# A hand-written order for three streams: six new lists, and a held period at the last image border

## The chip, the cores and the metric

The kernel runs on one core of one Trainium2 chip. The metric is the device time of one execution in microseconds; less is better. Engines are named as in the profile: PE (TensorE matmuls, with PEld for its weight loads), DVE (VectorE), ACT (ScalarE), POOL (GpSimd) and SP (SyncE, which here only issues DMAs).

## The reference

The input x is 4 images of 256 x 256 positions with 64 channels, float32. Layer 0 mixes in the frequency domain and then convolves; layer 1 works along the rows' axis (T = 256).

```python
h  = pw(ln(x, g1, b1), w_te, b_te)                      # 64 -> 128
F  = fft2(h, axes=(1, 2))
fc = gelu(pw(concat([real(F), imag(F)]), w_fc, b_fc))   # 256 -> 256
sp = real(ifft2(fc[..., :128] + 1j * fc[..., 128:], axes=(1, 2)))
x1 = x + pw(sp, w_tp, b_tp)                             # 128 -> 64
h2 = pw(ln(x1, g2, b2), w_fe, b_fe)                     # 64 -> 128
d  = gelu(depthwise3x3(h2, w_dw) + b_dw)
x2 = x1 + pw(d, w_fp, b_fp)                             # 128 -> 64
trend = moving_average(x2, 25)
xf = rfft(x2 - trend, axis=1)[:, :128]
ys = einsum('bmnc,cmk->bknc', xf, w_real + 1j * w_imag)
out = trend + irfft(pad(ys), n=256, axis=1)
```

## The kernel before

Layer 0 runs as three streams that overlap, each a few steps behind the one before it; what one image's stream leaves goes through DRAM to the next.

- The forward stream takes 32 column groups of each image: layer norm and the Fourier transform along the rows. Its operations are `fl` (load), `fq fr fR fm fM fA fB fC fp fx` (statistics, the root, scaling), `fa fb fh0 fh1` (sums and differences on DVE and POOL; `fh` is L609), `y0 y1` (transform on PE, L615), `yt0 yt1` (evictions on ACT and the store `y_d`).
- The spectral stream takes 65 row pairs of each image, two per period: `x xs` (second transform, L725 and L740), `m` (mixing matmuls with `wp`, L750), `gc b g` (copy on ACT L764, sums on DVE L770, activation on ACT L775), `p` (sums on POOL, L781), `z zs w zt` (product with `w_tp` and inverse transform, L805 to L833), `u us uc uf` (the inverse along the other axis, L856 to L920, and the store `u_d`, L896).
- The convolution stream takes 32 column chunks of each image: `ul UL xl XL cl` (loads), `c0 cc` (column sums on DVE; c0 is L990), `s` (inverse along the rows, L1041), `r0 r1` (residual, L1054 and L1062), `cq cr cR cm cM cA cB cC cp cx` (second layer norm; cx is L410), `t tt T Ta` (transpose and row sums; tt is L1098 to L1100 on ACT, T is L1124 to L1132 on POOL), the convolution's products, its combination, `a` (activation on ACT, L1276), `o fs ft st` (last product L1283, its eviction, the turn back L1308, residual and store).

The 3 x 3 convolution is done as six products over row and column combinations. `gm` issues the first of them (L1166): eight matmuls into two single PSUM banks `ps_h_c`, and then eight into a tile of two banks, `ps_hh_c`, of which there is one. `em` issues the rest: eight matmuls into two more single banks. `gh` and `eh` add the half-height products (L1180). The results are taken out by `gc_0 gc_1` (ACT, L1209 and L1212) and `cf0 cf1` (DVE, L1233 to L1245) for gm, and by `ec0 ec1` (ACT copies, L1200) with `sp0 sp1` (POOL sums, L1218 and L1223) for em. The last op of `cf1`, L1245, frees the two-bank tile. A chunk that comes late (`is_late`, from the period LATE_CHUNKS on) takes another path for em: `ce0 ce1`, DVE sums straight from PSUM (L1258, L1260). There are eight PSUM banks: six single ones, which are handed round between all operations in the order of issue, and the two-bank tile.

The order of work is written by hand and not left to a scheduler: PE, DVE, ACT and POOL run their instructions in exactly the order in which the program issues them, and SP issues the DMAs in that order. Before period S0 = 35, 17 turns of the list FIRST run the forward stream beside layer 1's matrix preparation (`v vc mm mt`, per-channel matrices that join moving average, transform and mixing). Then `period(n)` walks one list for n = 35 to 207: SPECTRUM to n = 71, FULL while all three streams run (72 to 131), MIXED when the forward stream has ended (132 to 170), and CONV when only the convolution remains (171 to 207). At the end `layer1` applies the matrices m_d to x2.

An entry `em:-4` means: issue `em` for chunk n - 4 in this period. `do(op, index)` first issues what the operation follows (FOLLOWS, EARLY) and what frees a bank for it, so an entry can pull others ahead of it, and one whose work was pulled before issues nothing. A chunk of the convolution has as its index the period in which it starts, given by `chunk_at`: 72 to 103 for the first image, 105 to 136, 137 to 168 and 170 to 201 for the others. At 104 and 169 there is no chunk, since an image's convolution needs the spectral stream's last rows; the empty index runs through the stages of the pipeline from period to period.

```python
    for b in range(B):
        at = max(at, S0 + opened(b) + 2 + LATE)
        for q in range(COLS):
            chunk_at[at] = (b, q)
            at += 1
    END = at + 6
```

Of the kernel before, what the change touches and what calls it, by code (L numbers as in the profile page):

```python
# [136 lines left out]
def conv_seq_kernel(ctx: ExitStack, tc: tile.TileContext, a: dict, tables: bass.AP, out: bass.AP):  # L137
    nc = tc.nc
    x = a["x"]
    B = x.shape[0]  # L140
# [27 lines left out]
    def make_room(op):  # L168

        for other in list(taken):  # L170
            if len(free_banks) >= NEEDS.get(op, 1):
                break
            if other in taken:
                holder, k = taken[other][1]
                late = holder == "em" and k >= LATE_CHUNKS
                releaser = "ce1" if late else RELEASES[holder]
                if (releaser, k) not in pulling:
                    pulling.append((releaser, k))
                    do(releaser, k)
                    pulling.pop()  # L180
# [1352 lines left out]
    S0 = FWD + 3  # L1533
    LATE = 1

    def opened(b):

        return (KH * (b + 1) + 2) // 2 + 1

    chunk_at, at = {}, 0  # L1540
    for b in range(B):
        at = max(at, S0 + opened(b) + 2 + LATE)
        for q in range(COLS):
            chunk_at[at] = (b, q)
            at += 1
    END = at + 6
    place = {chunk: at for at, chunk in chunk_at.items()}
    CONV_FROM = S0 + LATE + opened(B - 1) + 3

    def is_late(j):  # L1550
        return place[j] >= LATE_CHUNKS

# [42 lines left out]
    MIXED = numbered("""
        xl:-1 XL:-1 ft0:-6 zs:-5 st0:-6 ft1:-6 st1:-6 em:-4 g0:-3 T1:-3 Ta:-3 eh:-4 zt:-6 ec0:-4
        ec1:-4 m1:-3 sp0:-5 sp1:-5 cx:-2 w:-5 cf1:-5 gc1:-3 g1:-4 b1:-3 cm:-1 cc:-2 UL t0:-2 a0:-5
        xs:-1 zt:-5 gm:-4 t1:-2 tt0:-2 a1:-5 p0:-4 p1:-4 z:-4 zs:-4 gh:-4 uf:-3 cM:-1 p0:-3 gc_0:-4
        cf0:-4 g1:-3 cp:-1 m1:-2 gc1:-2 b1:-2 s cl tt1:-2 r0 gc_1:-4 m0:-2 gc0:-2 m0:-1 p1:-3 z:-3
        gc0:-1 r1 x b0:-2 xs o1:-5 fs1:-5 u:-2 o0:-5 T0:-2 x:1 cq b0:-1 us:-2 fs0:-5 g0:-2 cr cR  # L1600
        uc:-2 w:-4 ul:1
    """)

    CONV = numbered("""
        ce0:-5 ul:-1 s:-1 cl:-1 xl:-1 XL:-1 r0:-1 ce1:-5 r1:-1 a0:-5 ft0:-6 st0:-6 cr:-1 gm:-4
        ft1:-6 a1:-5 cq:-1 Ta:-3 cR:-1 o1:-5 o0:-5 gh:-4 st1:-6 t0:-2 gc_0:-4 fs0:-5 gc_1:-4 t1:-2
        cm:-1 cc:-2 cM:-1 cp:-1 cf0:-4 tt1:-2 cf1:-4 tt0:-2 em:-4 eh:-4 T0:-2 T1:-2 cx:-1 fs1:-5 UL
    """)
# [14 lines left out]
    PAIRS = set("x xs m0 m1 gc0 gc1 b0 b1 g0 g1 p0 p1 z zs w zt".split())
    BACK = {"u", "us", "uc", "uf"}
# [11 lines left out]
    def do(op, index):  # L1636

        if op not in ops:
            return
        for k in range(done.get(op, -1) + 1, index + 1):  # L1640
            for other, at in EARLY.get(op, ()) if k < LATE_CHUNKS else ():
                do(other, k + at)
            for other, at in follows.get(op, ()):
                do(other, k + at)
            if op in ("u", "zt") and ring[0](op, k):
                do(*ring[0](op, k))
            if op in ("fq", "cq", "cc") and sq_user:
                user = sq_user[-1][0]
                do(user, done[user[0] + "q"])
            if op in RELEASES:  # L1650
                make_room(op)
            if done.get(op, -1) >= k:
                continue
            done[op] = k
            busy.append((op, k))
            if op in PAIRS:
                if op == "x" and k < B * KH - 2:
                    do("yt0", (k + 3) // KH * FWD + FWD - 1)
                    do("yt1", (k + 3) // KH * FWD + FWD - 1)
                if k < B * KH:  # L1660
                    ops[op](k)
            elif op in BACK:
                ops[op](k)
            elif op in MATRICES:
                if k < C:
                    ops[op](k)
            elif op in HALF_MATRICES:
                if k < 2 * BESIDE:
                    ops[op](k)
            elif op in forward:  # L1670
                if k < B * FWD:
# [30 lines left out]
    with in_order, ExitStack() as right:  # L1702
        with (
# [3 lines left out]
            forward = forward_h(fwd)  # L1707
# [92 lines left out]
```

## Time and profile before

| | |
|---|---|
| median of 3 runs | 4286.83 us (4285.57 to 4288.68) |
| profiled execution | 4282.18 us |
| its span, first to last instruction | 4280.0 us |
| PE / DVE / ACT / POOL busy | 4123.3 / 3453.5 / 2962.3 / 3174.2 us |
| mean granted clock of PE | 0.987 |
| HBM traffic | 364.81 MB read, 286.00 MB written |

By stage (us from the start of the span; the border stages are those where one image's convolution gives way to the next):

| stage | from - to | length | PE busy |
|---|---|---|---|
| FIRST and fill | 0 - 340 | 340 | 304.0 |
| SPECTRUM | 340 - 780 | 440 | 437.8 |
| convolution comes in | 780 - 963 | 183 | 160.5 |
| FULL | 963 - 1628 | 665 | 660.0 |
| border at n = 104 | 1628 - 1852 | 224 | 205.1 |
| FULL | 1852 - 2381 | 529 | 526.7 |
| end of the forward stream, border at n = 137 | 2381 - 2577 | 196 | 183.1 |
| MIXED | 2577 - 3194 | 617 | 613.9 |
| last border | 3194 - 3419 | 225 | 187.8 |
| CONV | 3419 - 3798 | 379 | 376.7 |
| layer 1 | 3798 - 4280 | 482 | 467.7 |

A steady period takes 26.5 us in FULL, 23.6 in MIXED and 13.8 in CONV. In a row of the profile "x8" is the number of instructions in the group, the time in brackets is the idle time of that engine just before it, and the name after the arrow is what it waited for.

### The profile page before, as it was taken

How to read it: one execution, taken by the hardware profiler on the slowest of the kernel's cores; microseconds unless marked ns; L12 is line 12 of the kernel's file. 1: busy time of each engine (PE TensorE's matmuls, PEld its weight loads, DVE VectorE, ACT ScalarE, POOL GpSimd, SP SyncE). 2: the span in 40 equal slices, each digit the busy share in tenths (PEclk: the TensorE clock that was granted, in tenths of full speed). 3: DMA queues.
4: the chain of work that ended last, by engine and by line, in shares of the span. 5: the costliest groups of instructions: out<-in, count | busy, mean ns of one | idle time of the engine just before them, and what ended most of it. 6: DMA issues, size and time to landing. Idle time of an engine off the chain costs nothing.

```text
span 4280.0 us, 67389 instructions
## 1 busy us (share of the span) xinstructions
PE 4123.3 (96%) x22443; PEld 2329.5 (54%) x22443; DVE 3453.5 (81%) x5234; ACT 2962.3 (69%) x5409; POOL 3174.2 (74%) x3156
## 2 busy tenths in 40 slices
PE   8999999889999999899999999999998899999999
PEld 4544444345555555455555556666665566654444
DVE  6968999889999999899999878888886799962222
ACT  3438988778888887788888777888885466641221
POOL 6869999789999988899988877888886688840000
PEclk9999999999999999999999999999999999999999
DMA  6664555535555545445554333444433544439895
GB/s 192 213 192 132 158 159 165 170 99 138 139 138 138 138 138 141 125 132 140 141 141 133 100 106 101 110 108 123 109 99 101 165 114 114 118 109 368 344 342 226
DMA packets 763904, 655.26 MB, mean 153 GB/s; under 512 B 46413, under 2 KB 657695, under 8 KB 755240
## 3 DMA queue, kind: packets, MB, share of 16 engines
q1 hardware_dynamic: 726696, 583.84, 47.0%
q10 hardware_dynamic: 36864, 67.13, 4.1%
q8 instruction: 180, 2.95, 0.3%
q14 instruction: 164, 1.34, 0.1%
HBM read 364.81 MB, written 286.00 MB: 152 GB/s over the span
## 4 chain that ended last, share of the span: by engine, by line
PE 47%; DVE 8%; DMA 2%; POOL 2%; ACT 1%; issue 1%; SPq 0%; DVEq 0%; POOLq 0%; ACTq 0%
PE ps_o L1504 9%; PE ps_h_c L1166 5%; PE ps_p L750 4%; PE ps_h_c L1180 4%; PE ps_f_c L1283 4%; PE ps_s_c L1041 3%; PE ps_hh_c L1166 3%; PE ps_z L805 3%; PE ps_u L856 2%; PE ps_x L725 2%; PE ps_t_c L1088 2%; PE ps_ft_c L1308 2%; PE ps_hh_c L1180 2%; PE ps_zt L823 1%; PE ps_y L615 1%
## 5 line engine op out<-in xcount | busy, mean ns | idle before, releaser
L770 DVE TENSOR_TENSOR g<-ps_p,g 128x512 f32<-128x512 f32 x1040 | 703.0, 683 | 127.7 <-ACT g L764 109.4
L781 POOL TENSOR_TENSOR g<-g 128x512 f32<-128x512 f32 (+1 forms) x520 | 674.1, 1312 | 92.8 <-ACT g L775 84.9
L775 ACT ACTIVATE g<-g,b_fc 128x1024 f32<-128x1024 f32 (+1 forms) x520 | 595.2, 1145 | 1.7 <-DVE g L770 1.6
L750 PE MATMUL ps_p<-xs,wp 64*128 64x512 f32 (+1 forms) x2080 | 562.2, 615 | 7.0 <-DVE g L770 3.8
L1166 PE MATMUL ps_h_c<-td,wc_main 128*128 128x256 f32 x2048 | 500.5, 387 | 3.7 <-DVE g L770 1.4
L1504 PE MATMUL ps_o<-xc,mt 128*128 128x512 f32 x1024 | 441.2, 594 | 2.6 <-DVE oc L1518 2.6
L1166 PEld LDWEIGHTS ps_h_c<-td,wc_main 128*128 128x128 f32 x2048 | 372.6, 192 | 99.3 <-issue 32.1
L764 ACT COPY g<-ps_p 128x512 f32<-128x512 f32 (+1 forms) x520 | 298.5, 589 | 163.3 <-PE ps_p L750 80.7
L1276 ACT ACTIVATE h_c<-h_c,b_conv 128x1024 f32<-128x1024 f32 x256 | 296.5, 1160 | 158.1 <-DVE h_c L1245 53.8
L1518 DVE TENSOR_SCALAR oc<-ps_o,b_fp 128x512 f32<-128x512 f32 x128 | 93.6, 749 | 348.0 <-DMA out_dram<-oc 177.4
L1516 ACT ACTIVATE oc<-ps_o,b_fp 128x512 f32<-128x512 f32 x128 | 86.4, 686 | 359.4 <-PE ps_o L1504 202.8
L1128 POOL TENSOR_TENSOR td<-tt 128x512 f32<-128x512 f32 x256 | 326.9, 1298 | 10.0
L1504 PEld LDWEIGHTS ps_o<-xc,mt 128*128 128x128 f32 x1024 | 194.9, 191 | 248.3 <-issue 236.2
L609 POOL TENSOR_TENSOR xb<-xt 128x512 f32<-128x512 f32 x224 | 284.9, 1279 | 54.9 <-DVE xt L602 36.6
L750 PEld LDWEIGHTS ps_p<-xs,wp 64*128 64x128 f32 x2080 | 191.7, 186 | 235.7 <-issue 84.2
L805 PE MATMUL ps_z<-g,w_tp 128*64 128x512 f32 x1024 | 284.7, 616 | 25.8 <-POOL g L781 13.9
L1322 DVE TENSOR_TENSOR st<-x_c,ps_ft_c 128x256 f32<-128x256 f32 x512 | 260.5, 599 | 36.9 <-PE ps_ft_c L1308 36.8
L725 PEld LDWEIGHTS ps_x<-tab,yb 128*64 128x64 f32 x4064 | 232.7, 137 | 95.7 <-issue 38.3
L1180 PE MATMUL ps_h_c<-td,wc_half 64*128 64x256 f32 (+1 forms) x2048 | 278.9, 396 | 2.3 <-POOL td L1132 1.0
L615 PE MATMUL ps_y<-xb,tab 128*64 128x512 f32 x1024 | 270.6, 614 | 10.8 <-POOL xb L609 9.2
L1283 PE MATMUL ps_f_c<-h_c,w_fp 128*64 128x512 f32 x1024 | 266.1, 614 | 15.2 <-ACT h_c L1276 15.2
L1041 PE MATMUL ps_s_c<-uc_c,tab 64*128 64x512 f32 x1024 | 260.4, 612 | 16.6 <-DVE uc_c L990 11.2
(201 smaller groups left out, 9588.2 us busy)
## 6 DMA issues: line engine op xcount, KB each, us to landing
y_d<-yt SPq DMA_DIRECT2D x256, 256.0 KB, 3.6
yb<-y_d SPq DMA_DIRECT2D x256, 256.0 KB, 4.2
u_d<-ut SPq DMA_DIRECT2D x256, 256.0 KB, 3.6
x_c<-in_x_dram SPq DMA_DIRECT2D x512, 128.0 KB, 3.6
x_d<-st SPq DMA_DIRECT2D x128, 512.0 KB, 5.1
xc<-x_d SPq DMA_DIRECT2D x64, 1024.0 KB, 8.3
out_dram<-oc ACTq DMA_DIRECT2D x256, 256.0 KB, 5.7
xt<-in_x_dram SPq DMA_DIRECT2D x504, 128.0 KB, 2.5
```

What stands on the lines that cost most here:

```text
L725: nc.tensor.matmul(ps[r * C : (r + 1) * C, j * N + t * P : j * N + (t + 1) * P], blk[:, t, k, r * C : (r + 1) * C], tb[:, t, :], start=Tru ...
L750: nc.tensor.matmul(ps[:, :nf], wp[rows, cols], rhs[rows], start=True, stop=r == 1 or not pr["special"],)
L770: nc.vector.tensor_tensor(gt[:, i], re, gt[:, 1], op)
L775: nc.scalar.activation(g, g, AF.Gelu, bias=b_fc[:, half : half + 1])
L781: nc.gpsimd.tensor_tensor(g[:, 0], g[:, 0], g[:, 1], op)
L805: nc.tensor.matmul(ps[r * C : (r + 1) * C, :nf], w_tp, d[:, :nf], start=True, stop=True)
L1041: nc.tensor.matmul(pss[i], tb[i * C : (i + 1) * C], uc[i * C : (i + 1) * C, ::-1, 1 - r, :] if down else uc[i * C : (i + 1) * C, :, r, :], ...
L1128: tt_(new[:, k : k + 3 : 2], a_c, nb_e, op)
L1166: nc.tensor.matmul(product(j, k, par), wc_main[:, par, k, :], td[:, k, slots(j)].rearrange("p j q -> p (j q)"), start=k in (0, 1, 3), stop ...
L1180: nc.tensor.matmul(product(j, k, par)[:, dst.start * Q : dst.stop * Q], wc_half[lo : lo + C, k, :], td[lo : lo + C, k, src].rearrange("p j ...
L1283: nc.tensor.matmul(ps[par * C : (par + 1) * C], w_fp, gs[j][:, :, par, i0 : i0 + 2, :].rearrange("p r j q -> p r (j q)"), start=True, stop ...
L1504: nc.tensor.matmul(ps[:, :nf], mts[i // CM][:, i % CM, t, to * P : (to + 1) * P], xc[:, t, :, :, i, :], start=t == 0, stop=t == 1,)
```

## The change

The six lists are given in another order; most entries that move are not neighbours of what they were. Two things beside that: at n = 168 (HOLDS) the convolution is held for a period, which closes the gap at index 169, so that the last image's chunks are 169 to 200 and every convolution operation from n = 168 on uses n - 1 as its base; and LATE_CHUNKS becomes 166 for 167. END stays 208. A period's list in n = 168 then issues only what is left of the spectral stream.

On PE the order of FULL's instructions differs in one place: `em` of a chunk is issued ahead of `gm` of the same chunk and not after it. In MIXED and CONV it is as before, in SPECTRUM y0 and y1 change places. On the other engines: in FULL `cA` moves behind `zt` on ACT, the first pair of `p` ahead of `fh1` and `fx` ahead of `sp1` on POOL, `XL` ahead of `cl` on SP; in MIXED `Ta` and `xs` move earlier and one `zt` later on ACT, `sp0` ahead of `T1` on POOL, `ul` from the end of the period to its start on SP; in CONV `ft0` and `cR` move by a few places; in FIRST `fq`, `fR` and the `yt` stand elsewhere among ACT's. At n = 104 `UL:1` and `y1:-3` stand later in FULL, and so do `u`, `uc` and `uf` of two periods that they pull there.

```diff
+    HOLDS = [S0 + LATE + opened(B - 1)]
     chunk_at, at = {}, 0
     for b in range(B):
-        at = max(at, S0 + opened(b) + 2 + LATE)
+        at = max(at, S0 + opened(b) + 2 + LATE - sum(n <= S0 + opened(b) + 2 + LATE for n in HOLDS))
         for q in range(COLS):
             chunk_at[at] = (b, q)
             at += 1
-    END = at + 6
+    END = at + 6 + len(HOLDS)
...
     FULL = numbered("""
-        g1:-3 em:-4 b0:-2 ec1:-4 cm:-1 gh:-4 m0:-1 ec0:-4 fh1:-3 gc_0:-4 cf0:-4 a0:-5 g0:-2 m1:-1
-        p0:-3 fq:-1 p1:-3 z:-3 gc1:-1 fr:-1 gc0:-1 fs0:-5 o0:-5 o1:-5 b1:-1 fa:-3 fs1:-5 fh0:-3
-        b0:-1 y0:-3 ft0:-5 g1:-2 fR:-1 sp0:-4 cx:-2 w:-4 ft1:-5 st0:-5 zs:-3 p0:-2 fC:-3 yt0:-3
-        cc:-1 xl fm:-1 p1:-2 t1:-2 ul tt1:-2 sp1:-4 fp:-2 fM:-1 s cl fl t0:-2 w:-3 fA:-2 st1:-5
-        gc_1:-4 fx:-2 r0 XL tt0:-2 r1 cM:-1 uf:-3 zs:-2 gc1 T0:-2 T1:-2 m1 UL:1 fB:-2 y1:-3 cA:-1 cr
-        g0:-1 yt1:-3 u:-2 x:2 b1 zt:-4 us:-2 zt:-3 m0 xs:2 cf1:-4 z:-2 x:1 xs:1 gc0 a1:-4 Ta:-2
-        cB:-1 fb:-2 cq gm:-3 cC:-1 uc:-2 cR cp:-1 eh:-3
+        g1:-3 b0:-2 ec1:-4 cm:-1 gh:-4 m0:-1 cf0:-4 a0:-5 g0:-2 fC:-3 p0:-3 m1:-1 fq:-1 p1:-3 z:-3
+        ec0:-4 fh1:-3 fp:-2 gc1:-1 fr:-1 gc0:-1 gc_0:-4 o0:-5 fs0:-5 o1:-5 b1:-1 y0:-3 fa:-3 fs1:-5
+        fh0:-3 b0:-1 ft0:-5 g1:-2 fR:-1 sp0:-4 cx:-2 w:-4 ft1:-5 st0:-5 p0:-2 zs:-3 yt0:-3 cc:-1 xl
+        ul tt1:-2 fM:-1 s XL fm:-1 t0:-2 w:-3 st1:-5 p1:-2 t1:-2 cl fA:-2 fx:-2 fl gc_1:-4 r0 tt0:-2
+        r1 cM:-1 uf:-3 zs:-2 sp1:-4 m1 gc1 T0:-2 g0:-1 yt1:-3 u:-2 T1:-2 cr fB:-2 x:2 b1 cA:-1 zt:-4
+        us:-2 zt:-3 xs:2 z:-2 x:1 xs:1 gc0 em:-3 a1:-4 UL:1 y1:-3 Ta:-2 m0 fb:-2 cB:-1 cq gm:-3
+        cC:-1 cf1:-4 uc:-2 cR cp:-1 eh:-3
     """)
...
-    LATE_CHUNKS = CONV_FROM + max(at for op, at in MIXED if op in ("em", "gm"))
+    LATE_CHUNKS = (
+        CONV_FROM - len(HOLDS) + max(at for op, at in MIXED if op in ("em", "gm"))
+    )
...
     def period(n):
-        if any(n - k in chunk_at for k in range(7)):
+        if any(n - k in chunk_at for k in range(7 + len(HOLDS))):
             names = FULL if n < B * FWD + 4 else MIXED if n < CONV_FROM else CONV
         else:
             names = SPECTRUM
...
                 base = (n - S0 - HALF_MATRICES[op]) // 2
+            elif op not in forward:
+                base = n - sum(held <= n for held in HOLDS)
             do(op, base + at)
```

More of the change, by code (lines that the diff above doesn't have):

```diff
@@ L1593, in conv_seq_kernel @@
+        r1 cM:-1 uf:-3 zs:-2 sp1:-4 m1 gc1 T0:-2 g0:-1 yt1:-3 u:-2 T1:-2 cr fB:-2 x:2 b1 cA:-1 zt:-4
+        us:-2 zt:-3 xs:2 z:-2 x:1 xs:1 gc0 em:-3 a1:-4 UL:1 y1:-3 Ta:-2 m0 fb:-2 cB:-1 cq gm:-3
+        cC:-1 cf1:-4 uc:-2 cR cp:-1 eh:-3
     """)
     MIXED = numbered("""
-        xl:-1 XL:-1 ft0:-6 zs:-5 st0:-6 ft1:-6 st1:-6 em:-4 g0:-3 T1:-3 Ta:-3 eh:-4 zt:-6 ec0:-4
-        ec1:-4 m1:-3 sp0:-5 sp1:-5 cx:-2 w:-5 cf1:-5 gc1:-3 g1:-4 b1:-3 cm:-1 cc:-2 UL t0:-2 a0:-5
-        xs:-1 zt:-5 gm:-4 t1:-2 tt0:-2 a1:-5 p0:-4 p1:-4 z:-4 zs:-4 gh:-4 uf:-3 cM:-1 p0:-3 gc_0:-4
@@ L1599, in conv_seq_kernel @@
-        cf0:-4 g1:-3 cp:-1 m1:-2 gc1:-2 b1:-2 s cl tt1:-2 r0 gc_1:-4 m0:-2 gc0:-2 m0:-1 p1:-3 z:-3
-        gc0:-1 r1 x b0:-2 xs o1:-5 fs1:-5 u:-2 o0:-5 T0:-2 x:1 cq b0:-1 us:-2 fs0:-5 g0:-2 cr cR
-        uc:-2 w:-4 ul:1
+        xl:-1 sp0:-5 ft0:-6 zs:-5 st0:-6 XL:-1 ul ft1:-6 st1:-6 Ta:-3 em:-4 g0:-3 T1:-3 eh:-4 zt:-6
+        ec1:-4 cf1:-5 gc1:-3 cx:-2 b1:-3 cm:-1 ec0:-4 sp1:-5 cc:-2 xs:-1 w:-5 g1:-4 m1:-3 UL t0:-2
+        a0:-5 gm:-4 t1:-2 tt0:-2 a1:-5 p0:-4 p1:-4 zt:-5 zs:-4 gh:-4 cM:-1 p0:-3 uf:-3 cf0:-4
@@ L1602, in conv_seq_kernel @@
+        gc_0:-4 g1:-3 cp:-1 m1:-2 gc1:-2 b1:-2 s cl tt1:-2 r0 gc_1:-4 m0:-2 gc0:-2 m0:-1 p1:-3 z:-3
+        r1 x gc0:-1 xs fs1:-5 o1:-5 u:-2 z:-4 o0:-5 T0:-2 x:1 cq b0:-2 b0:-1 us:-2 fs0:-5 g0:-2 cr
+        cR uc:-2 w:-4
     """)
     CONV = numbered("""
-        ce0:-5 ul:-1 s:-1 cl:-1 xl:-1 XL:-1 r0:-1 ce1:-5 r1:-1 a0:-5 ft0:-6 st0:-6 cr:-1 gm:-4
-        ft1:-6 a1:-5 cq:-1 Ta:-3 cR:-1 o1:-5 o0:-5 gh:-4 st1:-6 t0:-2 gc_0:-4 fs0:-5 gc_1:-4 t1:-2
+        ce0:-5 ul:-1 s:-1 cl:-1 xl:-1 XL:-1 ft0:-6 r0:-1 ce1:-5 r1:-1 a0:-5 st0:-6 cr:-1 gm:-4
@@ L1607, in conv_seq_kernel @@
+        ft1:-6 a1:-5 cR:-1 cq:-1 Ta:-3 o1:-5 o0:-5 gh:-4 st1:-6 gc_0:-4 t0:-2 fs0:-5 gc_1:-4 t1:-2
         cm:-1 cc:-2 cM:-1 cp:-1 cf0:-4 tt1:-2 cf1:-4 tt0:-2 em:-4 eh:-4 T0:-2 T1:-2 cx:-1 fs1:-5 UL
     """)
-    LATE_CHUNKS = CONV_FROM + max(at for op, at in MIXED if op in ("em", "gm"))
+    LATE_CHUNKS = (
+        CONV_FROM - len(HOLDS) + max(at for op, at in MIXED if op in ("em", "gm"))
+    )
     FIRST = numbered("""
-        v:1 mm:-2 fl:1 fM fr fm y0:-2 y1:-2 v:2 mm fq:1 fx:-1 fp fh1:-1 fh0:-1 fm:1 vc:1 yt0:-2 fq:1
-        y1:-1 mt:-2 fx yt1:-2 fb:-1 mt:-3 fb mt fh1 yt0:-1 fp:1 vc:1 mm:-4 fa:-1 fr:1 fl:2 vc y0:-1
-        v:1 fR fR:1 yt1:-1 fh0:-1 fM:1 fa
+        v:1 fl:1 fM fr fm mm:-2 y0:-2 y1:-2 v:2 mm fx:-1 fp fh1:-1 fh0:-1 yt0:-2 fq:1 fx mt:-2
+        yt1:-2 y1:-1 fq:1 fm:1 vc:1 fb:-1 mt:-3 fb mt fh1 fa:-1 vc:1 mm:-4 fr:1 yt0:-1 fp:1 fl:2 vc
+        y0:-1 v:1 fR yt1:-1 fh0:-1 fR:1 fM:1 fa
@@ L1616, in conv_seq_kernel @@
     """)
     SPECTRUM = numbered("""
-        gc1:-1 yt0:-3 hm hv fr gc0:-1 x:1 uf:-1 p1:-1 z:-2 m0 xs:1 b0:-1 ht fm UL:1 y1:-2 x fx:-1
-        zs:-2 y0:-2 g0:-1 gc0 m1 hc b0 gc1 p1:-1 fR xs w:-2 zt:-2 fb:-1 m0 fq yt1:-2 p0:-1 fp fl:1
-        XL:1 zs:-1 fM z:-1 b1 fa:-1 fh1:-1 u fh0:-1 g0 us uc m1:1 w:-1 b1:1 g1 zt:-1 g1 p0
+        gc1:-1 yt0:-3 hv hm fr gc0:-1 x:1 uf:-1 p1:-1 z:-2 m0 xs:1 b0:-1 ht fm UL:1 y0:-2 g0:-1 gc0
+        fx:-1 y1:-2 x zs:-2 m1 p1:-1 hc b0 fR gc1 xs w:-2 zt:-2 fb:-1 m0 fq fl:1 XL:1 zs:-1 fM
@@ L1622, in conv_seq_kernel @@
+        yt1:-2 p0:-1 fp z:-1 b1 u fa:-1 fh1:-1 g0 us uc fh0:-1 b1:1 g1 zt:-1 m1:1 w:-1 p0 g1
     """)
```

## The prediction, made before the changed kernel ran

> **What bounds the kernel now.** I read the busy table and the slices of the page first, then cut the span into stages where the list or the load changes, then the chain of waits, the waits of a steady stretch, and last the order of time in one steady period and at the last border.
>
> ```profile
> PE 4123.3 (96%) x22443; PEld 2329.5 (54%) x22443; DVE 3453.5 (81%) x5234; ACT 2962.3 (69%) x5409; POOL 3174.2 (74%) x3156
> ...
> 780.00:963.00 183.00, 160.53 (x912) 78.81 (x912) 152.42 (x209) 136.28 (x255) 139.86 (x116) 0.96 0.45 128
> 963.00:1628.00 665.00, 659.96 (x4000) 380.82 (x3998) 629.14 (x931) 568.23 (x1093) 598.80 (x551) 1.00 0.51 140
> ...
> 2577.00:3194.00 617.00, 613.94 (x3947) 392.58 (x3945) 516.99 (x816) 509.14 (x876) 505.08 (x651) 1.00 0.41 110
> 3194.00:3419.00 225.00, 187.80 (x976) 121.82 (x976) 164.75 (x276) 120.25 (x225) 149.78 (x218) 0.92 0.44 129
> ```
>
> A stage row has the stretch in us and its length, then busy time of PE, PEld, DVE, ACT and POOL, clock, DMA share, GB/s. PE is the bound: the chain of waits gives it 47%, no other engine over 8%. The FULL stages (963 to 1628, and 1852 to 2381 with 526.7 of 529), MIXED (2577 to 3194) and CONV (3419 to 3798, 376.7 of 379) show it 99% busy, so moving other engines' work about there is worth nothing unless PE's own time shrinks. The PE time to be won lies at the phase-in (780 to 963, 22.5 us idle) and the last border (3194 to 3419, 37.2 us idle).
>
> Busy is not yet useful. A row is a run of instructions with its start, its length, and in brackets the idle time before it. PE and DVE at the turn of one FULL period, and the ACT row that opens the same chunk's evictions:
>
> ```profile
> 2083.45 1.99 PE L1166 MATMUL ps_h_c<-td,wc_main 128*128 128x256 f32 x8
> 2085.58 1.99 PE L1166 MATMUL ps_hh_c<-td,wc_main 128*128 128x256 f32 x8
> 2087.41 1.89 PE L1166 MATMUL ps_h_c<-td,wc_main 128*128 128x256 f32 x8
> ...
> 2084.84 0.68 DVE L1245 SCALAR_TENSOR_TENSOR h_c<-ps_hh_c,s_c 128x512 f32<-128x512 f32 x1
> ...
> PEld ps_hh_c L1166 <- DVE h_c L1245: 10.1, 20, 0.7
> ...
> 2063.86 1.07 ACT L1200 COPY h_c<-ps_h_c 128x512 f32<-128x512 f32 x2 [0.28 <-PE ps_h_c L1180]
> ```
>
> The line without a start is of the waits in 1852 to 2381 (total us, times, longest): the weight load of ps_hh waits for cf1 in all 20 periods. The two-bank pair tile is freed by the last op of cf1 (2085.52) and hh starts at 2085.58.
>
> **What the Trainium skill says.** "TensorEngine Tiling (Array Packing)", Key Properties: "Changing tiling mode (not just tile) drains the TensorE". The trace agrees: eight undisturbed products in a MIXED period take 1.73 us (2871.50 to the next start, 2873.23), here 1.83 up to the 64-row products, so 0.10 us. "TensorE: Matmul & The Clock Gate", What's actually happening: after an idle window of about 3.4 us the array runs at half clock. It agrees at the border, where granted clock falls to 0.77 and 0.76 and the eight matmuls of s take 3.79 us for some 2. "SBUF — State Buffer", Who interferes with whom: the port pair that VectorE and GpSimd share is an exclusive lock. It agrees: the POOL sum of L1125 takes 2.23 us beside the DVE sum of L920 and 1.28 in MIXED. So POOL's durations move with DVE's order, which I can't compute.
>
> **The change part by part.** Nearly the same instructions are issued: one more chunk takes the late path of its `em` results (two ACT copies and two POOL sums go, two DVE sums come), in CONV, where 17 us of DVE are idle over 379. Under 1 us; I take nothing.
>
> *FULL.* Of PE's order one thing changes: `em` (eight products, REST) stands ahead of `gm` (eight into single banks, then eight into the pair). Before, gm's singles to hh take 2085.58 − 2083.45 = 2.13 us: 1.73 of work, 0.40 lost, of which 0.10 I put down to the switch in from m0 (64 rows) and 0.30 to the wait for cf1; hh's restart costs up to 0.10 (1.83 for 1.73). With em first, hh starts at 2083.45 + 1.83 + 1.73 = 2087.01, 1.5 us after the pair is free, so the wait goes: 0.30 to 0.40 us of PE per period. What is late next? The loop through the others: eh on PE releases ec0 on ACT, whose evictions run to gc1, which releases b on DVE, then DVE is unbroken to cf1. In it only ACT's 0.28 us ahead of ec0 is idle for PE's sake. DVE (25.10 of 26.49 us busy in this period) can't shorten more than its waits on ACT. So I take 0.28, not 0.40. Steady periods: (665 + 529)/26.5 = 45. Gain 45 × 0.28 = 12.6, taken 13; ends 0 (other loops hold at 26.5) and 18 (45 × 0.40). The queue moves beside it are POOL's first p pair ahead of fh1, fx ahead of sp1, cA later on ACT, XL ahead of cl on SP: each keeps over half a us from its next user by the times of this period; nothing.
>
> The swap asks for banks earlier: em's come from zt and xs on ACT (done at 2081.83 and 2082.32, 1.1 us spare); gm's second single bank comes from the ACT copy gc0 (2084.07 + 0.59 = 2084.66), wanted at about 2085.5: 0.85 us spare.
>
> *Phase-in.* z on PE waits for p on POOL, because fh1 (1.27 us) runs on POOL between:
>
> ```profile
> 881.94 1.27 POOL L609 TENSOR_TENSOR xb<-xt 128x512 f32<-128x512 f32 x1
> 884.49 1.11 PE L805 MATMUL ps_z<-g,w_tp 128*64 128x512 f32 x1 [5.69 <-POOL g L781]
> ```
>
> The first p follows at 883.17. With p ahead, each such wait shrinks by 1.27. Four waits are 13.2 us in all; two or three have that fh1 in front: −3 (ends 0, −5).
>
> *First border between images (n=104).* The entries UL:1 and y1 come later, so what they pull (two periods of uc and uf on DVE, u:68 on PE) falls behind cf1 of chunk 100. The b and cf1 that PE waits for there (1.41 and 1.86 us) come sooner; the c0 of the next image comes later (2.34 us already). I take −1, ends −4 and +6. The border at n=137 keeps its stall, a chain of u_d through DRAM.
>
> *Last border.* Before, chunk 169 is a hole: every stage of the convolution passes an empty period in turn. After, the chunks are contiguous, and at n=168 all convolution work stands still for one period, with only `u` (about 1.7 us) on PE. Periods n = 169, 170, 173 and 174 before, and PE at n=173:
>
> ```profile
> 3278.00:3298.70 20.70, 16.79 (x80) 11.46 (x80) 11.34 (x21) 9.53 (x19) 12.29 (x20) 0.84 0.20 52
> 3298.70:3327.80 29.10, 19.02 (x81) 11.77 (x81) 15.71 (x23) 9.20 (x17) 19.27 (x19) 0.77 0.75 243
> ...
> 3355.60:3369.70 14.10, 8.32 (x36) 4.22 (x32) 10.94 (x19) 4.47 (x7) 10.78 (x14) 0.76 0.59 171
> 3369.70:3387.10 17.40, 14.10 (x74) 10.13 (x75) 12.10 (x20) 8.56 (x19) 13.67 (x23) 0.90 0.44 121
> ...
> 3364.51 1.12 PE L1283 MATMUL ps_f_c<-h_c,w_fp 128*64 128x512 f32 x2 [5.78 <-ACT h_c L1276]
> ```
>
> With the others (n=167 20.4, 168 20.1, 171 12.7, 172 15.1, 175 17.9, 176 13.9) the ten are 181.4 us for 144.4 of PE work. At n=170 s starts 21 us in, behind uf, its store, the load of `first` and c0; that chain stays. At n=173 the hole leaves PE 8.3 us of work in 14.1, and 5.78 us waiting for the activation. After, my estimate is n=167 20.4; 168 2.5 (u and its issue); 169 20.4; 170 29.1; 171 13.5; 172 15.1; and 173 to 176 at 14.2 each (steady CONV is 13.8): 157.8, so −23.6. That leaves 13 us of idle PE for 37. I take −20 since no trace shows the new overlap; ends −26 and +10 (if c0's chain starts a third later with less PE work ahead of it).
>
> SPECTRUM, MIXED, CONV and layer 1 keep PE's order and FIRST keeps DVE's bound, but for single swaps: nothing.
>
> Sum: −13 − 3 − 1 − 20 = −37. The profiled execution took 4282.18 us (span 4280.0), so 4245; the runs' median is 4.65 above it: 4286.83 − 37 = 4250.
>
> **The rivals.** *The swap is worth nothing, the hold works* (another loop, DVE with its POOL clashes, holds 26.5): −20: 4267. For it DVE 25.10 of 26.49; against it the 0.28 us on ACT. *The hold is worth nothing*: c0's chain stands later in CONV, where no spectral work covers it, only FULL and the phase-in count: −14 to −17, with the border's loss 4273. For it 5 us DMA legs at 75% DMA share; against it the hole's 5.78 us. *Slower*: gm's second bank. In FULL gc0 must follow both m0 and xs on ACT; if ACT's new order brings it over 0.85 us later, gm stalls after em, 0.4 us more than is saved, and the activations behind it slip: 48 × 0.4 = +19, less what the hold brings beyond its loss, 4301 with a hold of −5. For it 1.27 us of ACT waiting for ps_p just there; against it, that m0 itself doesn't move. *The change doesn't do what it says*: the hold only moves the bubble, and FULL's swap meets its loop: 4287.
>
> **How the numbers follow.** Forecast 0.43; swap worthless 0.21; hold worthless 0.14; nothing 0.07; slower 0.15. The forecast's own range is all ends together, 4233 to 4265, and 5 us lower for the clock at the border. The whole range goes from 4228 to 4290, leaving out the slower case and a small part below. No change means within 0.2%, 8.6 us. Of the hold-worthless case 0.02 falls within: faster 0.76, the same 0.09, slower 0.15.
>
> **What would show it.** FULL period 26.2 us, no wait of ps_hh for L1245, none of ps_h for L764; at the last border one period of some 2.5 us on PE, no 5.78 us wait, the ten periods near 158. A FULL period at 26.5 or above makes the first step wrong; a start of s over 21 us into n=170 with PE idle before it the last one.

## The result, and the profile after

| | before | after |
|---|---|---|
| median | 4286.61 us (4285.57 to 4288.68, 4 runs) | 4254.79 us (4248.27 to 4259.91, 4 runs) |
| ratio | | 0.9921, 95% interval 0.991 to 0.9933 |
| profiled execution | 4282.18 us | 4254.03 us |
| its span | 4280.0 us | 4252.2 us |
| clock | 0.987 | 0.988 |

The changed kernel is 32 us faster by the medians and 28 by the profiled executions; 37 had been forecast. That the total lies near the forecast says little of the working. Where the 28 us came from is read from one kind of mark in both traces: the start of the same matmul on PE at the end of each stretch (the spectral stream's x, L725, counted in steps of 32 matmuls, up to MIXED's end, then the convolution's s).

| stretch, up to this mark | before | after | gained here | forecast here |
|---|---|---|---|---|
| FIRST and fill: first x | 316.7 | 311.1 | 5.6 | 0 |
| SPECTRUM: 33rd x | 753.3 | 746.8 | 0.9 | 0 |
| phase-in: 44th x | 979.8 | 973.4 | −0.1 | 3 |
| first FULL stage: 65th x | 1536.7 | 1529.9 | 0.4 | 13 with the next FULL stage |
| border at n = 104: 77th x | 1868.8 | 1859.3 | 2.6 | 1 |
| second FULL stage: 95th x | 2345.9 | 2336.0 | 0.5 | |
| end of forward, border at n = 137: 106th x | 2643.8 | 2635.1 | −1.2 | 0 |
| MIXED: 128th x | 3165.1 | 3156.0 | 0.3 | 0 |
| last border: s of the last image's 9th chunk | 3446.5 | 3417.7 | 19.7 | 20 |
| CONV and layer 1: end | 4280.0 | 4252.2 | −0.9 | 0 |

The last border is as forecast. FULL, the second largest part of the forecast, gained nothing, and 5.6 us came from FIRST, to which nothing had been given. First the busy line of the page after, then its stages (columns as in the prediction), cut at the same marks shifted by what had been gained:

```profile
PE 4119.3 (97%) x22443; PEld 2342.4 (55%) x22443; DVE 3492.6 (82%) x5238; ACT 2951.0 (69%) x5407; POOL 3197.9 (75%) x3152
```

```profile
775.20:957.00 181.80, 163.02 (x906) 79.77 (x902) 151.79 (x205) 134.54 (x252) 137.57 (x115) 0.93 0.45 127
957.00:1622.00 665.00, 656.92 (x3992) 383.49 (x3990) 637.10 (x931) 565.11 (x1093) 598.60 (x551) 1.00 0.51 140
...
1843.50:2371.30 527.80, 522.74 (x3190) 304.81 (x3188) 502.74 (x733) 449.81 (x866) 476.93 (x440) 1.00 0.50 137
...
2568.20:3184.90 616.70, 615.66 (x3947) 396.41 (x3945) 528.56 (x816) 507.19 (x876) 525.34 (x650) 1.00 0.41 110
3184.90:3390.20 205.30, 182.20 (x976) 120.59 (x976) 166.48 (x281) 118.47 (x223) 150.99 (x213) 0.96 0.48 141
```

DVE's busy time rose by 39 us although it has only four instructions more; 8 of that lie in the first FULL stage, 7 in the second and 12 in MIXED. The first FULL stage has its old length with PE 3 us less busy; the second, which is cut 1.2 us shorter here (its gain by the marks is 0.5), has PE 4 us less busy. MIXED has its old length too. So the time that the swap freed on PE was not used.

**FULL.** The steady period is 26.50 us before and after (12 periods from s to s: 318.0 both times). PE, DVE and POOL of one period after:

```profile
2051.08 0.26 POOL L365 TENSOR_TENSOR rstd_c<-newton_c,seed_c 128x32 f32<-128x32 f32 x1 [0.43 <-ACT newton_c L364]
2052.15 0.49 POOL L376 TENSOR_TENSOR newton_c<-newton_c,var_c 128x32 f32<-128x32 f32 x1 [0.81 <-ACT newton_c L375]
2053.49 0.25 POOL L397 TENSOR_TENSOR rstd_c<-newton_c,rstd_c 128x32 f32<-128x32 f32 x1 [0.85 <-ACT newton_c L396]
...
2059.44 1.08 PE L1283 MATMUL ps_f_c<-h_c,w_fp 128*64 128x512 f32 x4 [0.32 <-ACT g L764]
...
2067.76 1.12 DVE L315 TENSOR_SCALAR seed_c<-var_c 128x32 int32<-128x32 int32 x1
...
2067.76 1.09 POOL L1124 TENSOR_TENSOR tt<-tt 128x512 f32<-128x512 f32 x1
...
2073.86 3.72 PE L1166 MATMUL ps_h_c<-td,wc_main 128*128 128x256 f32 x16
```

and the same DVE step before:

```profile
2077.36 0.73 DVE L315 TENSOR_SCALAR seed_c<-var_c 128x32 int32<-128x32 int32 x1
```

The waits of the second FULL stage after (us in total, times, longest) have no wait of ps_hh for L1245 any more. The weight load of ps_f, which waited for L764 before as well (15.5 us in total), waits longer, and PE itself now waits there too, which it did not before:

```profile
PEld ps_f_c L1283 <- ACT g L764: 22.3, 20, 1.2
PE ps_f_c L1283 <- ACT g L764: 5.0, 18, 0.3
```

The sixteen products of em and gm into single banks now run through (2073.86 to 2077.41), and hh starts at once behind them. But at 2059.44 PE waits 0.32 us at ps_f. And L315 on DVE lasts 0.39 us longer. It has not more to do: it ends at 2068.88, when POOL's L1124 ends (2068.85). What PE was given in one place it hands back in another, and the slack shows in DVE as busy time. POOL has no slack at all: 24.02 us busy in this period of 26.50, 2.09 us in the three waits of the root for ACT, and the rest in five gaps of some 0.08 us.

**Phase-in.** The two large waits of z fell from 4.54 and 5.69 us to 3.31 and 4.44, each by the length of the fh1 that no longer stands ahead. The waits of the stretch after:

```profile
PE ps_z L805 <- POOL g L781: 9.8, 3, 4.4
```

They were 13.2 us in all, so the 3 us that were forecast did come. But y on PE now waits for the fh1 that runs later (1.5 us in all for 0.2), the clock of the stretch is 0.93 for 0.96, and PE was busy 2.5 us longer for 906 matmuls than before for 912.

**Border at n = 104.** The waits for L770 and L1245 ahead of gm (1.41 and 1.86 us) are gone; what remains, in order of time:

```profile
1679.29 1.98 PE L750 MATMUL ps_p<-xs,wp 64*128 64x512 f32 x6 [1.09 <-DVE g L770]
1689.63 1.99 PE L1041 MATMUL ps_s_c<-uc_c,tab 64*128 64x512 f32 x8 [2.81 <-issue]
```

**Last border.** Cut from one chunk's s to the next. Before:

```profile
3251.20:3271.40 20.20, 15.69 (x90) 10.13 (x90) 14.73 (x24) 10.51 (x22) 14.42 (x21) 1.00 0.50 131
3271.40:3319.80 48.40, 34.92 (x172) 22.97 (x168) 28.52 (x46) 20.94 (x41) 29.11 (x35) 0.84 0.37 100
```

After:

```profile
3241.60:3265.20 23.60, 20.64 (x98) 12.95 (x96) 17.09 (x27) 10.97 (x23) 16.27 (x21) 0.86 0.52 134
3265.20:3290.60 25.40, 18.17 (x92) 11.55 (x88) 17.50 (x29) 12.26 (x25) 16.91 (x24) 0.90 0.40 108
```

The stretch that held the hole, 48.4 us with 34.9 of PE work, is 25.4 with 18.2; the one ahead of it is 3.4 longer. Of the waits of PE there, the one for c0 stays and the one for the activation shrinks:

```profile
3290.56 3.79 PE L1041 MATMUL ps_s_c<-uc_c,tab 64*128 64x512 f32 x8 [3.68 <-DVE uc_c L990]
...
3352.25 1.94 PE L1283 MATMUL ps_f_c<-h_c,w_fp 128*64 128x512 f32 x8 [3.81 <-ACT h_c L1276]
```

**FIRST.** The last turn before, on ACT and PE, and the first x:

```profile
286.02 1.07 ACT L633 COPY yt<-ps_y 128x512 f32<-128x512 f32 x2 [5.00 <-DMA y_d<-yt]
286.98 1.09 ACT L1414 COPY vs<-ps_v 128x512 f32<-128x512 f32 x2
287.64 3.42 PE L1421 MATMUL ps_m<-t,vs 128*128 128x256 f32 x8 [2.82 <-ACT vs L1414]
...
302.50 3.68 PE L615 MATMUL ps_y<-xb,tab 128*64 128x512 f32 x8 [4.56 <-POOL xb L609]
...
316.70 1.18 PE L725 MATMUL ps_x<-tab,yr 128*64 128x128 f32 x15
```

After:

```profile
280.16 1.07 ACT L633 COPY yt<-ps_y 128x512 f32<-128x512 f32 x2 [0.89 <-DMA y_d<-yt]
281.12 1.31 ACT L1414 COPY vs<-ps_v 128x512 f32<-128x512 f32 x2
281.64 3.62 PE L1421 MATMUL ps_m<-t,vs 128*128 128x256 f32 x16
...
296.70 3.68 PE L615 MATMUL ps_y<-xb,tab 128*64 128x512 f32 x8 [4.56 <-POOL xb L609]
...
311.14 1.18 PE L725 MATMUL ps_x<-tab,yr 128*64 128x128 f32 x15
```

There is one yt buffer, and its next eviction waits for the store of the last. Before, ACT waited 4 to 5 us for that store in nearly every turn of the list (69.1 us in 15 waits); after, one wait of 0.9 us is left. Inside FIRST this brings little: the y of the last turn starts at 278.99 before and at 277.95 after. In the last turn the matrix preparation stands right behind the held eviction: the copy vs (L1414) on ACT comes late, PE waits 2.82 us for it and runs the eight products of m behind the wait in 3.42 us, where the like group at 282.93 took 1.89. That delay goes on by way of m's eviction on DVE (L1432) and the statistics behind it (L294), the root and xb on POOL, to the y at 302.50, and from there PE runs without a wait to the first x. After, the wait for vs is gone, and y and x start 5.8 and 5.6 us earlier. The load yb, issued over 20 us ahead of x in both traces, is not what x waits for.

### The profile page after: what moved, and what is told of

It is laid out like the page before. It is cut to its first block, busy times and chain, and to the rows that moved or that the text cites. A ratio compares the mean times of both kernels' runs of the same rounds, so it can differ in the third digit from the quotient of the medians.

```text
span 4252.2 us, 67294 instructions
## 1 busy us (share of the span) xinstructions
PE 4119.3 (97%) x22443; PEld 2342.4 (55%) x22443; DVE 3492.6 (82%) x5238; ACT 2951.0 (69%) x5407; POOL 3197.9 (75%) x3152
## 4 chain that ended last, share of the span: by engine, by line
PE 63%; DVE 13%; ACT 10%; DMA 5%; POOL 4%; issue 3%; SPq 2%; ACTq 0%; DVEq 0%; POOLq 0%
PE ps_o L1504 9%; PE ps_p L750 8%; PE ps_h_c L1166 5%; PE ps_s_c L1041 5%; PE ps_f_c L1283 4%; PE ps_z L805 4%; PE ps_x L725 4%; PE ps_u L856 4%; PE ps_y L615 4%; PE ps_h_c L1180 3%; PE ps_hh_c L1166 3%; PE ps_zt L823 3%; PE ps_ft_c L1308 2%; PE ps_t_c L1088 2%; ACT sq L279 2%
## 5 line engine op out<-in xcount | busy, mean ns | idle before, releaser
L770 DVE TENSOR_TENSOR g<-ps_p,g 128x512 f32<-128x512 f32 x1040 | 703.0, 683 | 90.2 <-ACT g L764 72.0
L1166 PE MATMUL ps_h_c<-td,wc_main 128*128 128x256 f32 x2048 | 490.0, 387 | 1.4 <-ACT zs L813 0.6
L1166 PEld LDWEIGHTS ps_h_c<-td,wc_main 128*128 128x128 f32 x2048 | 374.8, 192 | 95.0 <-issue 33.6
L764 ACT COPY g<-ps_p 128x512 f32<-128x512 f32 (+1 forms) x520 | 297.6, 586 | 149.2 <-PE ps_p L750 90.9
L725 PEld LDWEIGHTS ps_x<-tab,yb 128*64 128x64 f32 x4064 | 233.6, 137 | 96.5 <-issue 45.9
```

The lines of the kernel that those rows point to most:

```text
L725: nc.tensor.matmul(ps[r * C : (r + 1) * C, j * N + t * P : j * N + (t + 1) * P], blk[:, t, k, r * C : (r + 1) * C], tb[:, t, :], start=Tru ...
L770: nc.vector.tensor_tensor(gt[:, i], re, gt[:, 1], op)
L1166: nc.tensor.matmul(product(j, k, par), wc_main[:, par, k, :], td[:, k, slots(j)].rearrange("p j q -> p (j q)"), start=k in (0, 1, 3), stop ...
```

## The experiments

### The parts, one by one

```diff
 e1_hold: before.py
+    HOLDS = [S0 + LATE + opened(B - 1)]
...
+            elif op not in forward:
+                base = n - sum(held <= n for held in HOLDS)
```

> The kernel before with the held period alone (chunks 169 to 200 for the last image, its lists unchanged). Theory: the emptied index was what cost at the last border, and nothing of it hangs on the new lists: the s of the last image's second chunk comes 20 us earlier and the time falls by 19 to 21 us, to about 4267. Rival: MIXED's and CONV's new places are needed to use the room; then under half of it, 4277 or more.

Measured: 4267.01 us, ratio 0.9958 (0.9946 to 0.9971). The s of the last image's second chunk starts at 3321.7 for 3340.4. By the medians the gain is 19.8 us, by the profiled executions 17.5. The hold pays nearly all of its 20 us without any of the new lists.

e2_full is the kernel before with only the FULL list of the diff.

> The kernel before with the new FULL list alone. Theory: the steady FULL period stays at 26.50 us, since something other than PE holds it there, and only the border at n = 104 gains some 3 us and the phase-in under 1: 4283, no more than 5 us below before. Rival (the prediction): 0.28 us for each of 45 periods, 13 us, 4273, which another of the new lists gave back in the changed kernel.

Measured: 4279.28 us, ratio 0.9986 (0.9979 to 0.9992). Steady period 26.49. In its trace the phase-in gives 2.6 us, the border at n = 104 3.4, and the end of the forward stream and the border at n = 137 another 2.1, which the changed kernel doesn't have. The whole, 7.5 us by the medians, is more than the 5 us that the theory allowed, but next to none of it is in the steady periods, where the prediction had put it.

e3_first is the kernel before with only the FIRST list of the diff.

> The kernel before with the new FIRST list alone. Theory: the last y_d stores of the first image go out 5 to 6 us earlier, so the first x of the spectral stream starts at 311 us in place of 317 and everything behind it moves by as much: 4281. Rival: the 5.6 us is one execution's chance in the DMA queues, and the time is within 2 us of before.

Measured: 4278.23 us, ratio 0.9981 (0.9973 to 0.9989), first x at 310.2 us. In every trace with the old list it starts between 316.7 and 319.6, in every one with the new between 309.3 and 312.4. The wait of PE for vs is 2.5 to 3.0 us in the former and absent in the latter. So the gain is no chance.

e12_three is the changed kernel with the lists MIXED, CONV and SPECTRUM of before.

> The changed kernel with the lists MIXED, CONV and SPECTRUM of before, so that the held period and the lists FULL and FIRST are all that is new. Theory: the parts add up (19.8, 7.5 and 8.5 us measured one by one), the three other lists bring nothing and cost up to 4 us at the borders: 4249 to 4256. Rival: the parts need the other lists to fit together at the border at n = 137 or at the last one: 4260 or more.

Measured: 4254.99 us, ratio 0.9925 (0.9912 to 0.9937), within its spread the changed kernel's time. MIXED, CONV and SPECTRUM together are worth nothing. The parts measured alone sum to 19.8 + 7.5 + 8.5 = 35.8 us, together they give 31.8; the intervals of the parts are wide enough for that.

### The swap alone

```diff
 e4_swap: before.py, FULL
-        g1:-3 em:-4 b0:-2
+        g1:-3 b0:-2
...
-        cB:-1 fb:-2 cq gm:-3
+        cB:-1 fb:-2 cq em:-3 gm:-3
```

> The kernel before with em moved directly ahead of gm in FULL and nothing else. Theory: the wait of ps_hh for L1245 goes (20 of 20 in the steady stretch to none), a new wait of about 0.3 us stands elsewhere on PE, the period stays at 26.50 and the time within 3 us of before. Rival (the prediction's step): period 26.2, 4273.

Measured: 4283.26 us, ratio 0.999 (0.9982 to 0.9998): 3.5 us by the medians, which its profiled execution doesn't show (1.3 us behind the old mark at the last border); steady period 26.50. The wait of ps_hh for L1245 is gone. The profile books no wait of PE at ps_f here, but the eight products of ps_f take 2.21 us up to the next group's start (2070.46) where they took 1.84 before (2069.95). This run's row, and that of the kernel before:

```profile
2068.25 2.38 PE L1283 MATMUL ps_f_c<-h_c,w_fp 128*64 128x512 f32 x8
2068.11 2.00 PE L1283 MATMUL ps_f_c<-h_c,w_fp 128*64 128x512 f32 x8
```

So the swap alone already gives back at ps_f what it frees at ps_hh.

### What holds the FULL period

If POOL's own queue holds it, work added there must lengthen it, and work added to DVE at a place where DVE has room must not.

```diff
 e10_pool: after.py
-            nc.gpsimd.tensor_tensor(t, a, s["var"][:, cols], ALU.mult)
+            for _ in range(2):
+                nc.gpsimd.tensor_tensor(t, a, s["var"][:, cols], ALU.mult)
...
 e9_dve: after.py, combine_first
-                    tt_(s[:, 0, par], s[:, 1, par], two, ALU.add)
+                    for _ in range(2 if place[j] < B * FWD and par == 0 else 1):
+                        tt_(s[:, 0, par], s[:, 1, par], two, ALU.add)
```

> The changed kernel with one small POOL product of the root (L355, 0.25 us by itself) issued twice in each FULL period. Theory: POOL holds the period, which grows by 0.2 to 0.25, 10 to 14 us in all. Rival: POOL's 2.1 us of waiting for ACT take it up, within 3 us of the changed kernel.

Measured: 4276.27 us, 21.5 over the changed kernel and about twice what was expected; steady period 26.92. Two successive periods on POOL, and PE's wait at ps_f, which grew from 0.32:

```profile
2041.26 0.29 POOL L366 TENSOR_TENSOR rstd_c<-newton_c,seed_c 128x32 f32<-128x32 f32 x1 [0.43 <-ACT newton_c L365]
2068.17 0.29 POOL L366 TENSOR_TENSOR rstd_c<-newton_c,seed_c 128x32 f32<-128x32 f32 x1 [0.43 <-ACT newton_c L365]
...
2076.30 1.08 PE L1284 MATMUL ps_f_c<-h_c,w_fp 128*64 128x512 f32 x4 [0.70 <-ACT g L765]
```

The product that takes 0.25 us by itself cost 0.42 a period: the pair lasted 1.36 us for 0.70, ending about where the sums of fa on DVE end, and a later step of the root (L377) took 0.25 for 0.49.

> The changed kernel with one DVE sum of cf0 (L1233, 0.41 us) issued twice for each chunk of the FULL stages (55 chunks). Theory: DVE waits at the port for POOL by about 0.7 us in each period, so that 0.41 more of its own is taken up there: period 26.5 to 26.6 and the time within 6 us of the changed kernel. Rival: DVE holds the period: 55 times 0.4, 20 us more.

Measured: 4250.12 us, not over the changed kernel, with 0.41 us more of DVE work in each of 55 chunks and a period of 26.49. So DVE's queue has room for 0.41 us at this place and is not what closes the period; DVE work behind the wait that took it up was not tried. The place where I had looked for its room was wrong: L315 still lasts 1.13 us, and it is the wait of b for gc1 (11.6 us in 20 periods of the changed kernel) that took the sum up. The waits of the second FULL stage in e9:

```profile
DVE g L770 <- ACT g L764: 3.8, 3, 1.6
```

### Taking work off POOL

```diff
 e7_edge: after.py, add_sums (e8_edge_old: the same in before.py)
-                nc.gpsimd.tensor_tensor(
-                    ends, ends, edge_rows[:, k : k + 1].to_broadcast([P, 2 * NP]), ALU.add
-                )
+                nc.scalar.activation(ends, ends, AF.Identity, bias=edge_rows[:, k : k + 1])
```

> The changed kernel with the two edge sums of sp0 (L1223, 0.38 us per chunk) done by ACT and no longer by POOL; the result is the same. Theory: POOL's queue with its waits for ACT holds the FULL period at 26.50, so 0.3 us or so of each period goes until PE (26.2) holds it: 12 to 16 us, 4239 to 4243, and DVE's seed step L315, which in the changed kernel lasts 1.12 us for 0.73 since it stands behind POOL at the port, gets shorter. Rival: DVE itself, or the loop from ec0 through gc1, b and cf1, holds the period; then nothing, or ACT's 0.4 us more makes it longer: 4255 to 4272.

Measured: 4257.13 us, no gain. The trace shows why: the FULL period fell to 26.35 and the kernel stood 12.9 us ahead of the changed one at the 106th x; in MIXED, where the same entry stands elsewhere in ACT's order, the period rose from 23.6 to 24.0, the lead was 4.4 us at the 128th x, and 1.0 after the last border.

> The kernel before with the edge sums moved to ACT in the same way, em still behind gm. Theory: POOL holds the period here as well, and the wait for cf1 at ps_hh has some 0.3 us of room, which is hidden in DVE's waits at the port: the period falls by 0.2 to 0.3, 9 to 14 us, a little less than with em ahead. Rival: the loop through ps_hh and cf1 holds it, within 3 us of before.

Measured: 4439.86 us, ratio 1.0353 (1.0339 to 1.0368). In FULL the period is 26.41, a gain of 0.09 for 0.15 with em ahead. Nothing of the loss is FULL's: in the old MIXED list sp1 follows sp0 at once, so that POOL waits for ACT's edge sum, and the period is 28.2. The waits from 2600 to 3100:

```profile
POOL h_c L1218 <- ACT h_c L1223: 75.9, 16, 4.8
```

e11_edge_full moves the edge sums for the chunks of FULL alone (`if place[j] < B * FWD`).

> The changed kernel with the edge sums on ACT for the chunks of the FULL stages alone; after them POOL does them as before. Theory: with POOL's queue 0.38 us shorter the FULL period is 26.33, as it was with the edge sums on ACT throughout, while MIXED is back at 23.57: 7 to 8 us for the steady FULL periods, 12 to 14 with the phase-in and the border at n = 104, so 4241 to 4248, faster than both. Rival: the steady periods' gain is given back at the borders, as MIXED gave it back: 4253 or more.

Measured: 4245.24 us (4241.58 to 4245.3), ratio to before 0.9898 (0.9883 to 0.9913): 9.6 us under the changed kernel's median and the fastest of all. Two successive periods on DVE, and POOL in the second:

```profile
2056.56 0.63 DVE L315 TENSOR_SCALAR seed_c<-var_c 128x32 int32<-128x32 int32 x1
2082.91 0.63 DVE L315 TENSOR_SCALAR seed_c<-var_c 128x32 int32<-128x32 int32 x1
...
2082.42 1.09 POOL L1124 TENSOR_TENSOR tt<-tt 128x512 f32<-128x512 f32 x1 [0.24 <-ACT tt L1099]
```

L315 is back from 1.12 to 0.63 us, POOL now waits for ACT in one more place, and the stretch's row shows PE busy without a gap:

```profile
2056.56:2082.91 26.35, 26.35 (x162) 15.77 (x161) 24.98 (x38) 23.23 (x47) 23.69 (x21) 1.00 0.56 156
```

That row does not mean that PE alone holds the period now. The eight products of s last longer than in the changed kernel (second row), and ACT's edge sums and the eviction behind them stand beside them:

```profile
2078.39 2.23 PE L1041 MATMUL ps_s_c<-uc_c,tab 64*128 64x512 f32 x8
2063.24 1.99 PE L1041 MATMUL ps_s_c<-uc_c,tab 64*128 64x512 f32 x8
...
2077.63 0.49 ACT L1224 ACTIVATE h_c<-h_c,edge_rows 128x8 f32<-128x8 f32 x2
2078.02 0.56 ACT L813 COPY zs<-ps_z 128x512 f32<-128x512 f32 x1
```

The second bank's first weight load for s starts at 2078.64, 0.05 us after L813 ends, and so it does in all twelve periods looked at, in e7 and e8 too; in the changed kernel it starts 0.2 us after. The sums moved to ACT make L813 late, and PE waits for it inside a row that looks busy. From one matmul's start to the next, summed by group, PE spends (us a period, means of 12):

| | before | after | e4 | e10 | e8 | e11 |
|---|---|---|---|---|---|---|
| em and gm into single banks (L1166) | 3.92 | 3.56 | 3.56 | 3.56 | 3.65 | 3.56 |
| last product, ps_f | 1.84 | 2.22 | 2.22 | 2.63 | 1.83 | 1.84 |
| s | 1.92 | 1.92 | 1.92 | 1.92 | 2.15 | 2.16 |
| all others | 18.82 | 18.81 | 18.81 | 18.81 | 18.78 | 18.81 |
| period | 26.50 | 26.50 | 26.50 | 26.92 | 26.41 | 26.36 |

In each kernel one group (in e8 two) is longer than in the others. The smallest figures of the lines sum to 26.1, an estimate of the period that PE by itself could hold; no run reached it. In e8 the wait at ps_hh is mostly gone (3.65) with em still behind gm: it was for the larger part a consequence of POOL's queue.

The second way was to keep POOL's work and fill its waits for ACT in the root:

```diff
 e5_root: after.py, FULL (e6_root_old: the same moves in before.py)
-        u:-2 T1:-2 cr fB:-2 x:2 b1 cA:-1 zt:-4
+        u:-2 cA:-1 T1:-2 cr fB:-2 x:2 b1 zt:-4
...
-        gc0 em:-3 a1:-4 UL:1 y1:-3 Ta:-2 m0 fb:-2 cB:-1 cq gm:-3
-        cC:-1 cf1:-4 uc:-2 cR cp:-1 eh:-3
+        gc0 em:-3 cB:-1 a1:-4 UL:1 y1:-3 Ta:-2 m0 fb:-2 cC:-1 cq gm:-3
+        cf1:-4 uc:-2 cR p0:-1 cp:-1 eh:-3
```

> The changed kernel with the steps of the joint root spread on POOL in FULL: its first product ahead of T1, the second step's ACT part ahead of the activation, the third ahead of the next square, and one p between the last two. Theory: POOL's own queue with its three waits for ACT in the root (0.43, 0.81 and 0.85 us) is what holds the FULL period at 26.50; with two of them covered the period falls to where PE alone holds it, 26.1 to 26.2, some 13 to 18 us in all, and PE's 0.3 us wait at ps_f goes. Rival: ACT and DVE hold it (ec0 to gc1 to b to cf1), or the clock of PE itself; then the period stays at 26.5 and the time within 3 us of the changed kernel.

Measured: 4253.88 us, within its spread the changed kernel's time; period 26.43. Two of POOL's three waits in the root went and the third fell to 0.36 us, but a new one came in every period, and on DVE the sums of fb (L602), which lasted 1.29 us, now run beside a p on POOL. Waits of 1860 to 2280, and one row:

```profile
POOL h_c L1218 <- DVE s_c L1233: 12.9, 16, 0.8
```

```profile
2072.91 2.37 DVE L602 TENSOR_TENSOR xt<-xb 128x512 f32<-128x512 f32 x2
```

DVE has no booked wait left in this period (26.03 us busy in 26.50). So here, by the trace alone, DVE holds it: the move bought POOL's time with DVE's.

> The kernel before with the same spreading of the root in its FULL list, em still behind gm. Theory: here PE's wait for cf1 at ps_hh is a second loop of about the same length (26.4 to 26.5), so the spreading alone is worth little: within 5 us of before, where with em ahead of gm it is worth 13 to 18. Rival: the order of em and gm has no part in it and the gain is the same in both.

Measured: 4272.73 us, ratio 0.9969 (0.9957 to 0.998). The steady period is 26.44, as in e5. But 14 us were gained where at most 5 had been expected, with em still behind gm: by the marks of its profiled execution, 4.2 come from the phase-in, 5.9 from the borders at n = 104 and n = 137, and 2.9 from the FULL stages. The theory of two loops of equal length in the kernel before fell; what the moves do at the borders was not followed further.

## Why the prediction was right or wrong

- *The last border: −20, measured −19.7 (−19.8 alone).* Right in mechanism: the emptied place was what cost. The c0 chain stayed (3.68 us for 3.62), and the hole's wait for the activation went from 5.78 to 3.81 us, not to nothing, as had been listed. The working itself came to 23.6, and the step from there to 20 was a judgement; that it fits to 0.3 us is in part luck. The rival in which the hold is worth nothing is out.
- *FULL: −13, measured −0.9 over 39 steady periods.* This is the step that failed, in the sentence "In it only ACT's 0.28 us ahead of ec0 is idle for PE's sake". What the swap does on PE was right: the wait for cf1 went in every period. What is late next was looked for on ACT and DVE only. POOL, 24.0 us busy of 26.5, was not followed round its period: its idle time is the root's steps, passed to ACT and back one after another, and behind the last of them its queue is unbroken up to the next. That loop is 26.5 us long, before and after, and PE gave back at ps_f what it had been given (0.38 us for 0.36). e10 shows that the period follows POOL (0.42 us more), e7, e8 and e11 that it falls once POOL has less although ACT has more, which excludes ACT, and e9 that DVE's queue has room. The first rival of the prediction gave the right outcome, the swap worth nothing. It named DVE with its POOL clashes: DVE's own queue has room by e9, but the clashes are part of POOL's length, by some 1.6 us a period, an estimate from L1125 (2.23 for 1.28), L355 (0.70 for 0.25) and L376 (0.49 for 0.25).
- *"Moving other engines' work about there is worth nothing"* was read from PE's 99% and is wrong for FULL: e11 moves 0.38 us of POOL's work and takes 0.15 from each period. A row that looks busy can hold waits of up to 0.4 us (ps_f in e4).
- *The end of 18 us for that step* supposed that PE alone would run at 26.1. No run shows that period, and none excludes it: the 26.35 of e11 has 0.24 us of waiting for ACT in it. With the edge sums on ACT in both, e8 against e7 puts the swap's worth at 0.06 us a period.
- *Phase-in: −3, measured 0.1 the other way.* The waits shrank by 1.23 and 1.25 us, as worked out (1.27), but y's wait for the later fh1 and a lower clock stood against it. With the same FULL list the stretch gave 2.6 us in e2 at a clock of 0.97, 1.2 in e12 and −0.1 in e9, both at 0.95; how much of it is the clock's stays open.
- *n = 104: −1, measured −2.6 (3.4 in e2).* Right in kind: the waits named are gone, and the wait ahead of s grew from 2.34 to 2.81.
- *FIRST: nothing, measured −5.6 (8.5 by the medians of e3).* The term was missing. "FIRST keeps DVE's bound" holds for its turns and not for the last one, where ACT's wait for the one yt buffer made vs late, and through vs PE, DVE, POOL and the first x.
- *SPECTRUM, MIXED, CONV: nothing.* e12 agrees within its spread (by the marks the new SPECTRUM list gives 0.9 us).
- *Slower through gm's second bank*: no wait of ps_h for L764 comes in FULL; excluded.
- *The range.* Its upper end, 4265, is not "all ends together": the upper ends of the four terms (0, 0, +6, +10) give 4303; the lower ones give 4234, one more than stated.

Of the 37 us that were forecast, 12 in FULL and 3 in the phase-in did not come, and 8 that were not forecast came (5.6 in FIRST, 1.6 more at n = 104, 0.9 in SPECTRUM); the other stretches took some 2 back. That the total came out near is luck. By the medians the fall is 4 us larger than by the profiled executions; the times of the changed kernel spread over 11 us, so its 32 is known to some 5.

## What to carry to other kernels

When every engine's row is nearly full, look for the loop that closes on itself: follow each engine's queue round one period, and count a wait that is a hand-over to another engine and back as part of the loop and not as slack. Then test it: add a little work on one engine at a time, not just ahead of a wait that takes it up; the engine that holds the period passes it on. A row without gaps is no proof that its engine holds the period: compare the time from a group's start to the next one's between two runs, and see what ends where the longer one starts. A stage bounded in its turns by one engine can still end on another chain, here a wait for a single buffer with other work behind it in the same queue, so a reordering of it is priced there as well. And an emptied place in a pipeline is paid in every stage that it passes.

## What the runs showed of the hardware

- Waiting at the port that DVE and POOL share is booked as busy time of the waiting instruction: L315 lasted 0.44 (e5), 0.63 (e11), 0.73 (before) or 1.12 us (after) for the same 32 elements a partition, and each time it ended within 0.05 us of POOL's L1124. The Trainium skill, "SBUF — State Buffer", Who interferes with whom, has it that a tensor_scalar too can contend for the shared pair, in its two-port modes; the durations agree, though no trace shows the mode. So a full row can hide slack: with POOL's queue shorter, DVE's busy time in a period fell from 25.50 to 24.98 us with the same work (e11). PE's rows hide waits too: the eight products of s lasted 2.23 us for 1.99 with no gap booked, while they waited for a bank (e11).
- A small POOL product's price depends on its neighbour on DVE: L355 took 0.26 us in e5, 0.70 beside the sums of L582 before and after, and 0.42 a period when added a second time (e10).
- A hand-over from POOL to ACT and back cost POOL 0.43 us with one small activation between, 0.81 with a square of 1.05 us ahead of it on ACT, and 0.85 with two small activations.
